# Values projected head by head, with the expert bias added as they leave PSUM

## The chip, the cores and the metric

The kernel runs on one core of a Trainium2 chip. The metric is the device time of one execution in microseconds (us), the median of several runs. A core has five engines that matter here: TensorE (PE) for matrix products and transposes, VectorE (DVE) and ScalarE (ACT) for elementwise work and for emptying PSUM, GpSimd (POOL) for elementwise work between tiles in SBUF, and SyncE (SP), which issues DMAs. Each engine has its own queue of instructions, and they meet at semaphores.

## The reference

A small vision tower: a tokenizer, attention with relu differences, an attention whose projections belong to experts, linear attention, and routed experts. The change is in the third. For 128 images (B) of 64 tokens (T) with 256 features (D), split into four chunks of 64 features, each chunk goes through four experts (e) with two heads each:

```python
gate = softmax(xn @ router_w.T + router_b)
qkv  = einsum('btcd,ekd->btcek', xc, qkv_w)          # xc: xn in four chunks c of 64
attn = softmax(einsum('bcehtd,bcehsd->bcehts', q, k) * scale)
y    = einsum('bcehts,bcehsd->bcehtd', attn, v)       # heads h side by side: 64 wide
y    = einsum('btced,eod->btceo', y, proj_w) + proj_b # proj_b: one bias per expert
out  = einsum('btceo,bte->btco', y, gate)
return residual + out.reshape(B, T, D) @ out_w.T
```

So the bias of expert e enters once, times the gate of e. The softmax weights of a head sum to one over the tokens s. A bias that is added to the values of one of the two heads of an expert therefore comes out of that head's sum as the same bias, and the gate that multiplies the weights multiplies it too.

## The kernel before

`expert_attention` works on pairs of images: 64 pairs, 128 tokens on the partitions, in blocks of four pairs. All tensors are fp32. The projection matrices are folded into the value matrices at the start (`wvp`), so that what leaves the mixing of the heads (`pz`) is already projected. The softmax weights are multiplied by the gates on POOL (`weights`, L987), so that the sum over the experts is made in PSUM by the four products that accumulate into one place of `pz`.

The loop over pairs is software-pipelined, and its order is written out by hand under `manual_schedule`: every engine takes its instructions in the order of the program's text. In step p three pairs are in work: `old` (p - 1) is transposed, mixed and added to the output; `cur` (p) gets its scores and its softmax; `new` (p + 1) gets queries, keys and values. In PE's order one step is: the first transposes of the old pair (L1001), the scores of the current one (L965), queries and keys of the new one (L933) with the old pair's other transposes between, the mixing `pz` (L1014), the values `pv` (L945), the output product `po` (L1028), and last the block work of the step. DVE takes in one step: for each of two halves of the scores a maximum (L977) and a subtraction (L978), then for each half a sum (L984) and a reciprocal (L985), with small work of the block between, then the copies of the values that are its own (L954), and last the addition of `po` to the running state `h2` (L1030). ACT copies queries and keys (L937), the transposed weights (L1004), makes the exponents (L981), copies `z` (L1022) and its share of the values (L954). POOL scales the weights (L991, L992) and normalises coming blocks (L866, L869).

The block work is put in the steps by `at`: a coming block's statistics are in DVE's part of the steps with p mod 4 of 1 and 2, the transposes of its normalised rows (L874) in PE's part of the steps 0 and 1, its router logits (L885) in step 2, the softmax of its gates (L892 to L904) in step 3.

[...] Two tiles of two banks are the scores; the other four banks are the pool `psq`, tag `pq`, in which everything else takes turns: a new tile takes the bank that was given back the longest ago. In one step they are taken in this order: two `pt`, two `pqk`, two `pt`, two `pqk`, `pz`, two `pv`, two `pv`, `po`, and then the tile of the block work, if the step has one.

Before the change, `values(fc)` makes the values of both heads for one half `fc` of the features, two tiles each time, with products of 256 columns. ACT copies those of `fc` 0, DVE those of `fc` 1. The bias takes a way of its own: the start of the stage multiplies it by `out_w` (`pb`, L819) and lays the result out in `bn`, four rows for each pair of a block; the gates of a block are transposed by PE (L908), copied by ACT into one of three `gT` tiles (L911), and each pair adds a third product to `po`:

```python
nc.tensor.matmul(po, self.blk.gT, bn[:, self.n, :], start=False, stop=True)
```

PE executes an fp32 product as two records in the trace, and a transpose as one.

Of the kernel before, what the change touches and what calls it, by code (L numbers as in the profile page):

```python
# [11 lines left out]
F32 = mybir.dt.float32  # L12
# [7 lines left out]
P = 128  # L20
B = 128
T = 64
D = 256
# [737 lines left out]
def expert_attention(c, hd, normw, wr, br, wqkv, wvT, wproj, bproj, wout):  # L761
# [3 lines left out]
    tc, nc, h2 = c.tc, c.nc, c.h2  # L765
    SCALE = float(1.0 / np.sqrt(np.float32(32)))
    NP = B // 2
    NB = 4
    with (
# [12 lines left out]
        brs = wp.tile([P, 4], F32, name="brs")  # L782
        nc.sync.dma_start(brs, br.partition_broadcast(P))
        w = wp.tile([P, 2 * D], F32, name="w")
        bp2 = wp.tile([P, 4], F32, name="bp2")
        for k in range(2):
            nc.sync.dma_start(w[k * 64 : k * 64 + 64, :], wqkv)
            nc.sync.dma_start(bp2[k * 64 : k * 64 + 64, :], bproj)
        wv = wp.tile([32, 8, 64], F32, name="wv")
        nc.scalar.dma_start(wv, wvT)  # L790
        wpj = wp.tile([32, 8, 64], F32, name="wpj")
# [10 lines left out]
        for k in range(2):  # L802
            for e in range(4):
                for h in range(2):
                    r = (e % 2 * 2 + h) * 64
                    nc.tensor.matmul(
                        pv[k * 64 : k * 64 + 64, e // 2, r : r + 64],
                        wv[:, e * 2 + h, :],
                        wpj[:, e * 2 + h, :],
                        start=True,  # L810
                        stop=True,
                    )
        wvp = wp.tile([P, 2, D], F32, name="wvp")
        nc.vector.tensor_copy(wvp, pv)


        pb = psq.tile([4, D], F32, tag="pq", name="pb")
        for fc in range(2):
            nc.tensor.matmul(pb, bp2, wo[:, fc, :], start=(fc == 0), stop=(fc == 1))  # L819
        b4 = wp.tile([4, D], F32, name="b4")  # L820
        nc.vector.tensor_copy(b4, pb)
        bn = wp.tile([P, NB, D], F32, name="bn")
        nc.gpsimd.memset(bn, 0.0)
        for n in range(NB):
            nc.sync.dma_start(bn[4 * n : 4 * n + 4, n, :], b4)
        gTs = [wp.tile([P, P], F32, name=f"gT{k}") for k in range(3)]
        for gT in gTs:
            nc.gpsimd.memset(gT, 0.0)

        class Block:  # L830

            def __init__(self, p0):
                self.p0, self.gT = p0, gTs[p0 // NB % 3]

            def statistics(self, n0):
                if n0 == 0:
# [63 lines left out]
            def gates(self):  # L903
                nc.gpsimd.tensor_mul(self.gate, self.gate, bcast(self.gm, 2, 4))  # L904

            def gates_transpose(self):
                self.pgt = psq.tile([4 * NB, P], F32, tag="pq", name="pgt")
                nc.tensor.transpose(self.pgt, self.gate.rearrange("p n e -> p (n e)"), c.ident)  # L908

            def gates_transposed(self):  # L910
                nc.scalar.copy(self.gT[0 : 4 * NB, :], self.pgt)  # L911

        class Pair:


            def __init__(self, p, blk):
                self.p, self.n, self.blk = p, p % NB, blk
                self.xT = blk.xT[:, :, p % NB, :]
                self.e, self.sm, self.pT = {}, {}, {}

                self.qk = vp.tile([P, 4, 2, 2, P], F32, tag="qk", name="qk", bufs=2)

                self.v = vp.tile([P, 4, 2, D], F32, tag="v", name="v")

            def queries_keys(self, fc):

# [9 lines left out]
                for par in range(2):  # L936
                    nc.scalar.copy(self.qk[:, 2 * fc + par], pq[par])  # L937

            def values(self, fc):
                pv = [psq.tile([P, 2, D], F32, tag="pq", name="pv") for _ in range(2)]  # L940
                for j in range(2):
                    for eh in range(2):
                        for par in range(2):
                            r = slice(par * 64, par * 64 + 64)
                            nc.tensor.matmul(  # L945
                                pv[par][eh * 64 : eh * 64 + 64, j, :],
                                self.xT[r, fc, j * 64 : j * 64 + 64],
                                wvp[r, eh, :],
                                start=True,
                                stop=True,  # L950
                            )
                for par in range(2):
                    copy = nc.scalar.copy if fc == 0 else nc.vector.tensor_copy
                    copy(self.v[:, 2 * fc + par], pv[par])  # L954

            def scores(self):

# [48 lines left out]
            def mixed(self):  # L1006

                pz = psq.tile([P, 2, P], F32, tag="pq", name="pz")
                for fc in range(2):
                    for j in range(2):  # L1010
                        t = slice(j * 64, j * 64 + 64)
                        for r in range(4):
                            for par in range(2):
                                nc.tensor.matmul(  # L1014
                                    pz[par * 64 : par * 64 + 64, fc, t],
                                    self.v[:, 2 * fc + par, j, r * 64 : r * 64 + 64],
                                    self.pT[r // 2][:, r % 2, 2 * fc + par, t],
                                    start=(r == 0),
                                    stop=(r == 3),
                                )  # L1020
                self.z = ep.tile([P, 2, P], F32, tag="z", name="z", bufs=2)
                nc.scalar.copy(self.z, pz)  # L1022

            def output(self):
                p = self.p
                po = psq.tile([P, D], F32, tag="pq", name="po")
                for fc in range(2):
                    nc.tensor.matmul(po, self.z[:, fc], wo[:, fc, :], start=(fc == 0), stop=False)  # L1028
                nc.tensor.matmul(po, self.blk.gT, bn[:, self.n, :], start=False, stop=True)
                nc.vector.tensor_add(h2[:, p], h2[:, p], po)  # L1030
                if p % 4 == 3:
                    nc.sync.dma_start(
                        hd[2 * p - 6 : 2 * p + 2].rearrange("(n b) t f -> (b t) n f", b=2),
                        h2[:, p - 3 : p + 1],
                    )
# [5 lines left out]
        def at(n, place, f, *a):  # L1041
            key = (n, place) if n >= 0 else "first"
            work.setdefault(key, []).append(lambda: f(*a))

        for b, x in enumerate(blocks):
            n = NB * b
            at(n - 11, "DVE", x.statistics, 0)
            at(n - 10, "DVE", x.statistics, 2)
            at(n - 9, "POOL", x.factors)
            for k in range(NB):  # L1050
                at(n - 8 + k, "POOL", x.normal, k)
            at(n - 4, "PE", x.transpose, 0)
            at(n - 3, "ACT", x.transposed, 0)
            at(n - 3, "PE", x.transpose, 1)
            at(n - 2, "ACT", x.transposed, 1)
            at(n - 2, "PE", x.logits)
            at(n - 1, "DVE", x.logits_less_max)
            at(n - 1, "ACT2", x.exponents)
            at(n - 1, "DVE2", x.sums)
            at(n - 1, "POOL", x.gates)  # L1060
            at(n, "PE", x.gates_transpose)
            at(n + 1, "ACT", x.gates_transposed)

        def do(key):
            for step in work.pop(key, ()):
# [3 lines left out]
        with tc.manual_schedule():  # L1069
            old, cur = None, Pair(0, blocks[0])  # L1070
            for fc in range(2):
                cur.queries_keys(fc)
                cur.values(fc)
            for p in range(NP):
                new = Pair(p + 1, blocks[(p + 1) // NB]) if p + 1 < NP else None
                do((p, "ACT"))
                if old:
                    old.transposed(0)
                cur.scores()
                cur.less_max(0)  # L1080
                cur.less_max(1)
                if new:
                    new.queries_keys(0)
                if old:
                    old.transposed(1)
                cur.exponents(0)
                if new:
                    new.queries_keys(1)
                cur.exponents(1)
                cur.sums(0)  # L1090
                cur.weights(0)
                do((p, "DVE"))
                do((p, "ACT2"))
                cur.sums(1)
                cur.weights(1)
                do((p, "DVE2"))
                do((p, "POOL"))
                if old:
                    old.mixed()
                if new:  # L1100
                    new.values(0)
                    new.values(1)
                if old:
                    old.output()
                do((p, "PE"))
                old, cur = cur, new
            for x in range(2):
                old.transposed(x)
            old.mixed()
            do((NP, "ACT"))  # L1110
            old.output()
        assert not work

# [873 lines left out]
def layout(**i):  # L1987
# [32 lines left out]

    o["wvf"] = w[:, 2].reshape(8, 32, 64).transpose(1, 0, 2)
    o["wproj"] = i["L0_ffn_proj_w"].reshape(4, 64, 2, 32).transpose(3, 0, 2, 1).reshape(32, 8, 64)
    o["bproj"] = i["L0_ffn_proj_b"].T
    o["wout"] = i["L0_ffn_out_w"].T

    q, k, v = (i[f"L1_attn_W{n}"].T.reshape(D, 8, 32).transpose(0, 2, 1).reshape(D, D) for n in "qkv")
# [29 lines left out]
```

## Time and profile before

What | us
--- | ---
median of 3 runs | 2745.43 (2745.28 to 2745.86)
the profiled execution | 2744.63
its span, first to last instruction | 2742.5
PE busy in the span | 2598.4 (95%)
DVE, ACT, POOL busy | 2027.9, 1623.1, 1633.7
stage of this change, about 1139 to 1942 | 803
PE busy over 1400 to 1900, in its middle | 494.87 of 500

A row of the profile's groups gives line, engine, operation, the tiles out and in, the number of instructions, then busy time and mean duration, and last the idle time of the engine before them. A row of the timeline gives start, duration, engine, line and operation, and merges like neighbours. A row of the waits says which engine at which line waited for which other, how long in total, how often, and the longest. PEld is PE's weight load, which runs beside the products.

### The profile page before, as it was taken

Reading aid. Unit: us, or ns where it says so; the run is one execution under the profiler, and the core shown is the slowest. Engines: PE = TensorE matmul, PEld = TensorE weight load, DVE = VectorE, ACT = ScalarE, POOL = GpSimd, SP = SyncE. Lnnn points to the kernel's source line nnn. Section 1 sums busy time; section 2 is a strip of 40 time slices with the busy share of each in tenths; the row PEclk is TensorE's granted clock in tenths of the full one; section 3 lists DMA queues with packets and bytes.
Section 4 is the critical chain, followed back from the end, with each engine's and each line's share of the span. In section 5 each row is a group of like instructions: output and inputs, shape, how many; then the busy total and the mean of one; then the engine's idle time right before and its main releaser. Section 6 shows DMA issues by size and latency. Waiting matters only on the chain. (4 is left out here: it accounts for less than half of the span.)

```text
span 2742.5 us, 77026 instructions
## 1 busy us (share of the span) xinstructions
PE 2598.4 (95%) x33309; PEld 1733.3 (63%) x33309; DVE 2027.9 (74%) x3025; ACT 1623.1 (59%) x3414; POOL 1633.7 (60%) x1390
## 2 busy tenths in 40 slices
PE   7989999999999999799999999999699986999997
PEld 4553444444344443588888888888466565888886
DVE  5759999999998989477777777777467776444443
ACT  2228888888888888366656666666355543233332
POOL 3328888888888889656566656553233212454444
PEclk9999999999999999899999999999899998999998
DMA  3000000000000000000000000000333454555554
GB/s 109 32 12 1 2 1 2 2 2 2 1 2 1 2 2 1 12 11 19 11 11 19 11 11 18 11 12 17 96 83 85 100 118 149 179 198 197 184 195 134
DMA packets 138015, 140.83 MB, mean 51 GB/s; under 512 B 107747, under 2 KB 121461, under 8 KB 129984
## 3 DMA queue, kind: packets, MB, share of 16 engines
q1 hardware_dynamic: 126928, 117.95, 14.2%
q0 software_dynamic: 7648, 14.77, 1.7%
q8 instruction: 263, 4.31, 0.6%
q10 hardware_dynamic: 3088, 3.08, 0.4%
q14 instruction: 88, 0.72, 0.1%
HBM read 103.96 MB, written 32.54 MB: 50 GB/s over the span
## 5 line engine op out<-in xcount | busy, mean ns | idle before, releaser
L525 POOL TENSOR_TENSOR m<-q,k 128x1024 f32<-128x1024 f32 x384 | 719.0, 1904 | 31.7 <-PE sc L327 16.3
L517 DVE TENSOR_TENSOR m<-pc,k 128x2048 f32<-128x2048 f32 (+1 forms) x320 | 646.7, 2058 | 0.5 <-ACT q L461 0.5
L327 PE MATMUL sc<-m,wide 128*32 128x512 f32 x4096 | 529.7, 599 | 12.0 <-DVE m L517 7.1
L526 ACT ACTIVATE m<-m 128x1024 f32<-128x1024 f32 x384 | 402.5, 1050 | 5.9 <-POOL m L525 5.4
L327 PEld LDWEIGHTS sc<-m,wide 128*32 128x32 f32 x4096 | 126.6, 109 | 259.6 <-issue 146.2
L535 ACT ACTIVATE m<-k,q 128x64 f32<-128x64 f32 x1024 | 271.0, 339 | 0.8 <-DVE k L408 0.8
L977 DVE TENSOR_REDUCE mx<-sc 128x16 f32<-128x1024 f32 x128 | 156.0, 1219 | 153.2 <-PE sc L965 138.1
L992 POOL TENSOR_TENSOR e<-e,mx 128x1024 f32<-128x1024 f32 x128 | 243.4, 1902 | 10.1 <-POOL mx L991 0.2
L937 ACT COPY qk<-pqk 128x512 f32<-128x512 f32 x256 | 139.0, 604 | 132.2 <-PE pqk L933 132.1
L991 POOL TENSOR_TENSOR mx<-mx,gate 128x16 f32<-128x16 f32 x128 | 27.6, 216 | 314.8 <-ACT z L1022 144.3
L1886 PE MATMUL ph<-xt,w1s 128*128 128x256 f32 x896 | 198.8, 380 | 3.6 <-DVE xt L1877 2.6
L1902 PE MATMUL po<-w2s,hT 128*128 128x256 f32 x896 | 198.0, 379 | 0.0
L1004 ACT COPY pT<-pt 128x512 f32<-128x512 f32 x256 | 138.6, 599 | 99.0 <-PE pt L1001 98.3
L1886 PEld LDWEIGHTS ph<-xt,w1s 128*128 128x128 f32 x896 | 169.8, 190 | 28.2 <-DVE xt L1877 3.2
L1902 PEld LDWEIGHTS po<-w2s,hT 128*128 128x128 f32 x896 | 168.1, 190 | 21.7
L933 PE MATMUL pqk<-xT,w 64*128 64x128 f32 x2048 | 169.6, 289 | 3.7 <-issue 3.5
L978 DVE TENSOR_TENSOR e<-sc,mx 128x1024 f32<-128x1024 f32 x128 | 156.7, 1224 | 4.4
L1920 POOL DMA_INDIRECT out<-y,rout x56 | 56.7, 1013 | 167.8 <-ACT hT L1890 124.8
L933 PEld LDWEIGHTS pqk<-xT,w 64*128 64x128 f32 x2048 | 142.3, 189 | 21.1 <-issue 12.0
L984 DVE TENSOR_REDUCE mx<-e 128x16 f32<-128x1024 f32 x128 | 153.3, 1198 | 2.1 <-ACT e L981 2.0
L1890 ACT ACTIVATE hT<-ph,w1s 128x256 f32<-128x256 f32 x224 | 93.0, 470 | 96.9 <-PE ph L1886 96.9
L1001 PE MATMUL pt<-ident,e 128*128 128x128 f32 x1024 | 141.5, 278 | 5.8 <-POOL e L992 2.8
(308 smaller groups left out, 4958.7 us busy)
## 6 DMA issues: line engine op xcount, KB each, us to landing
w1s<-in_we SPq DMA_DIRECT2D x30, 1028.0 KB, 5.0
w2s<-in_we SPq DMA_DIRECT2D x30, 1024.0 KB, 5.2
hd<-h SPq DMA_DIRECT2D x16, 512.0 KB, 3.4
x<-hd SPq DMA_DIRECT2D x16, 512.0 KB, 5.7
h<-hd SPq DMA_DIRECT2D x4, 2048.0 KB, 12.6
hx<-h SPq DMA_DIRECT2D x4, 2048.0 KB
out<-h SPq DMA_DIRECT2D x4, 2048.0 KB, 20.6
xt<-in_x SPq DMA_DIRECT2D x15, 512.0 KB, 3.5
```

The costliest lines, as they stand in the source:

```text
L327: nc.tensor.matmul(dst[j : j + 32], wide[:, hf, s : s + 32], part, start=start, stop=stop)
L517: nc.vector.tensor_tensor(m, bcast(self.pq[:, hf, i : i + n], 3, T), k, ALU.max)
L525: nc.gpsimd.tensor_tensor(m, bcast(self.q[:, hf, s : s + 2], 3, T), k, ALU.subtract)
L526: nc.scalar.activation(m, m, AF.Relu)
L535: nc.scalar.activation(self.parts[i, hf][:, q], self.blk.k[:, hf, i], AF.Relu, bias=self.q[:, hf, i - NB // 2, q : q + 1], scale=-1.0,)
L933: nc.tensor.matmul(pq[par][:, k, eh, :], w[r, f : f + P], self.xT[r, fc], start=True, stop=True)
L977: nc.vector.tensor_reduce(mx, sc, AX.X, ALU.max)
L978: nc.vector.tensor_sub(e, sc, bcast(mx, 2, T))
L984: nc.vector.tensor_reduce(self.sm[x], self.e[x], AX.X, ALU.add)
L992: nc.gpsimd.tensor_mul(e, e, bcast(sm, 2, T))
L1886: nc.tensor.matmul(ph[:, j], self.w1[:, w0 : w0 + P], self.xt[:, fc], start=(fc == 0), stop=(fc == 1))
L1902: nc.tensor.matmul(po, self.hT[:, f, r * P : r * P + P], self.w2[:, f, :], start=(f == 0), stop=(f == 7))
```

## The change

The values are made head by head. The folded value matrix `wvp` is laid out with head 0 of all experts in its first 128 columns and head 1 in the others, and `values(h)` makes one head for both halves of the features, two tiles each time, with twice as many products of half as many columns. The value tile in SBUF has a new order of its axes, and the mixing reads it accordingly. The two tiles of head 0 leave PSUM by DVE, as an addition of the bias `bv`; the two of head 1 by ACT, as copies. `bv` is loaded by two DMAs in place of the two of `bp2`: each expert's bias broadcast over the 64 partitions that hold that expert's tokens. Gone are the transposes of the gates, their copies, `gT`, `bn`, `b4`, the products `pb`, the four DMAs that fill `bn`, and the third product of `po`.

```diff
-        bp2 = wp.tile([P, 4], F32, name="bp2")
+        bv = wp.tile([P, P], F32, name="bv")
         for k in range(2):
             nc.sync.dma_start(w[k * 64 : k * 64 + 64, :], wqkv)
-            nc.sync.dma_start(bp2[k * 64 : k * 64 + 64, :], bproj)
+            nc.sync.dma_start(
+                bv[k * 64 : k * 64 + 64, :],
+                bproj[2 * k : 2 * k + 2].rearrange("e o -> (e o)").partition_broadcast(64),
+            )
...
-                    r = (e % 2 * 2 + h) * 64
+                    r = (h * 2 + e % 2) * 64
...
-        pb = psq.tile([4, D], F32, tag="pq", name="pb")
-        for fc in range(2):
-            nc.tensor.matmul(pb, bp2, wo[:, fc, :], start=(fc == 0), stop=(fc == 1))
-        b4 = wp.tile([4, D], F32, name="b4")
-        nc.vector.tensor_copy(b4, pb)
-        bn = wp.tile([P, NB, D], F32, name="bn")
-        nc.gpsimd.memset(bn, 0.0)
-        for n in range(NB):
-            nc.sync.dma_start(bn[4 * n : 4 * n + 4, n, :], b4)
-        gTs = [wp.tile([P, P], F32, name=f"gT{k}") for k in range(3)]
-        for gT in gTs:
-            nc.gpsimd.memset(gT, 0.0)
...
-            def gates_transpose(self):
-                self.pgt = psq.tile([4 * NB, P], F32, tag="pq", name="pgt")
-                nc.tensor.transpose(self.pgt, self.gate.rearrange("p n e -> p (n e)"), c.ident)
-
-            def gates_transposed(self):
-                nc.scalar.copy(self.gT[0 : 4 * NB, :], self.pgt)
...
-                self.v = vp.tile([P, 4, 2, D], F32, tag="v", name="v")
+                self.v = vp.tile([P, 2, 2, 4, P], F32, tag="v", name="v")
...
-            def values(self, fc):
-                pv = [psq.tile([P, 2, D], F32, tag="pq", name="pv") for _ in range(2)]
-                for j in range(2):
-                    for eh in range(2):
-                        for par in range(2):
-                            r = slice(par * 64, par * 64 + 64)
-                            nc.tensor.matmul(
-                                pv[par][eh * 64 : eh * 64 + 64, j, :],
-                                self.xT[r, fc, j * 64 : j * 64 + 64],
-                                wvp[r, eh, :],
-                                start=True,
-                                stop=True,
-                            )
+            def values(self, h):
+                pv = [psq.tile([P, 4, P], F32, tag="pq", name="pv") for _ in range(2)]
+                for fc in range(2):
+                    for j in range(2):
+                        for eh in range(2):
+                            for par in range(2):
+                                r = slice(par * 64, par * 64 + 64)
+                                nc.tensor.matmul(
+                                    pv[par][eh * 64 : eh * 64 + 64, 2 * fc + j, :],
+                                    self.xT[r, fc, j * 64 : j * 64 + 64],
+                                    wvp[r, eh, h * P : h * P + P],
+                                    start=True,
+                                    stop=True,
+                                )
                 for par in range(2):
-                    copy = nc.scalar.copy if fc == 0 else nc.vector.tensor_copy
-                    copy(self.v[:, 2 * fc + par], pv[par])
+                    if h == 0:
+                        nc.vector.tensor_add(self.v[:, par, 0], pv[par], bcast(bv, 1, 4))
+                    else:
+                        nc.scalar.copy(self.v[:, par, 1], pv[par])
...
-                                    self.v[:, 2 * fc + par, j, r * 64 : r * 64 + 64],
+                                    self.v[:, par, r % 2, 2 * fc + j, r // 2 * 64 : r // 2 * 64 + 64],
...
-                    nc.tensor.matmul(po, self.z[:, fc], wo[:, fc, :], start=(fc == 0), stop=False)
-                nc.tensor.matmul(po, self.blk.gT, bn[:, self.n, :], start=False, stop=True)
+                    nc.tensor.matmul(po, self.z[:, fc], wo[:, fc, :], start=(fc == 0), stop=(fc == 1))
...
-            at(n, "PE", x.gates_transpose)
-            at(n + 1, "ACT", x.gates_transposed)
...
-            do((NP, "ACT"))
```

The loop itself still calls `new.values(0)` and then `new.values(1)`, after `old.mixed()` and ahead of `old.output()`.

More of the change, by code (lines that the diff above doesn't have):

```diff
@@ L814, in expert_attention @@
         nc.vector.tensor_copy(wvp, pv)
-        pb = psq.tile([4, D], F32, tag="pq", name="pb")
-        for fc in range(2):
-            nc.tensor.matmul(pb, bp2, wo[:, fc, :], start=(fc == 0), stop=(fc == 1))
-        b4 = wp.tile([4, D], F32, name="b4")
-        nc.vector.tensor_copy(b4, pb)
-        bn = wp.tile([P, NB, D], F32, name="bn")
-        nc.gpsimd.memset(bn, 0.0)
-        for n in range(NB):
-            nc.sync.dma_start(bn[4 * n : 4 * n + 4, n, :], b4)
-        gTs = [wp.tile([P, P], F32, name=f"gT{k}") for k in range(3)]
-        for gT in gTs:
-            nc.gpsimd.memset(gT, 0.0)
         class Block:
             def __init__(self, p0):
-                self.p0, self.gT = p0, gTs[p0 // NB % 3]
+                self.p0 = p0
             def statistics(self, n0):
@@ L2022, in layout @@
     o["wproj"] = i["L0_ffn_proj_w"].reshape(4, 64, 2, 32).transpose(3, 0, 2, 1).reshape(32, 8, 64)
-    o["bproj"] = i["L0_ffn_proj_b"].T
+    o["bproj"] = i["L0_ffn_proj_b"]
     o["wout"] = i["L0_ffn_out_w"].T
```

## The prediction, made before the change was run

> **What bounds the kernel now.** I read the page's slices first, then busy time by stage, then the waits, then one pair in the timeline. The expert attention runs from about 1139 to 1942 us of the span. In its steady part TensorE (PE) is busy 494.9 of 500 us at the full granted clock; VectorE (DVE) 386.4, ScalarE (ACT) 309.6, GpSimd (POOL) 285.1. The columns are stretch, length, then PE, PE weight loads, DVE, ACT, POOL, clock, DMA share, GB/s:
> ```profile
> 1400.00:1900.00 500.00, 494.87 (x11375) 418.32 (x11373) 386.39 (x554) 309.58 (x561) 285.11 (x315) 1.00 0.04 14
> ```
> So PE's own queue is the bound, and 1% of slack is left. What decides the change is how near other engines stand to PE at the place that it touches. The waits of this stage name that place:
> ```profile
> PEld po L1028 <- ACT v L954: 23.5, 61, 0.4
> DVE mx L977 <- PE sc L965: 137.9, 57, 3.7
> ```
> The first line: in 61 pairs the output product `po` takes the PSUM buffer that the first value tile leaves. `psq` has four, and the order of use is `pz`, four value tiles, `po`. It costs nothing yet (0.4 us of weight loads, in which PE drains the values' products anyway). The second: DVE waits each pair for the scores, so DVE's chain begins anew at each pair's scores, and nothing carries over. One pair (number 32), from the values to the next scores:
> ```profile
> 1544.91 2.10 PE L945 MATMUL pv<-wvp,xT 64*64 64x256 f32 x32
> 1545.47 0.39 ACT L1022 COPY z<-pz 128x256 f32<-128x256 f32 x1
> 1545.57 0.25 DVE L985 RECIPROCAL mx<-mx 128x16 f32<-128x16 f32 x1
> 1545.74 1.16 DVE L984 TENSOR_REDUCE mx<-e 128x16 f32<-128x1024 f32 x1
> ...
> 1546.05 1.07 ACT L954 COPY v<-pv 128x512 f32<-128x512 f32 x2 [0.19 <-PE pv L945]
> ...
> 1546.93 1.13 PE L1028 MATMUL po<-wo,z 128*128 128x256 f32 x4
> 1546.94 0.25 DVE L985 RECIPROCAL mx<-mx 128x16 f32<-128x16 f32 x1
> 1547.11 1.23 DVE L954 COPY v<-pv 128x512 f32<-128x512 f32 x2
> ...
> 1547.90 0.59 PE L1029 MATMUL po<-bn,gT 128*128 128x256 f32 x2
> ...
> 1548.33 0.27 PE L908 MATMUL pgt<-ident,gate 128*16 128x128 f32 x1
> ```
> ACT empties the first two value tiles from 1546.05, 0.9 us before `po` starts. DVE comes to its two only at 1547.11, after the second sum and reciprocal: later than `po`'s start. Today that is harmless, since `po` doesn't ask for those.
>
> **What the Trainium skill says.** "TensorE: Matmul & The Clock Gate", section "Part 2: What happens when you issue a matmul": matmuls stay in program order, only weight loads are pulled ahead. So everything behind a waiting `po` waits too; the trace agrees, since the transposes of the next pair start only after L1029. The same page, Part 1 ("What's actually happening"): the clock is halved after an idle window of some 3.4 us. PE has such idle at this stage's start, where the granted clock over 1112 to 1139 is 0.62; in the loop it is 1.00. "VectorE: DVE Perf Modes", "The perf-mode tier table": an fp32 tensor_tensor, or any fp32 operation with a PSUM operand, gets no faster mode. The trace agrees: L499, an fp32 add of 128x512 from PSUM, takes 0.677 us, the copies at L954 0.662.
>
> **The change, part by part.**
>
> *Removed from PE.* A record of 256 columns takes 0.216 us of PE's time: the two of L1029 start at 1547.90 and the next instruction at 1548.33, 0.43 for both. There are 64 such products: 64 x 0.432 = 27.6 us. The 16 gate transposes take 0.11 each (1548.33 to 1548.44): 1.7. Together 29.4 us of PE.
>
> *Values by head.* Before: 32 records of 256 columns in four 64x64 quarters of the array, 8 rounds x 0.216 = 1.73 us. After: 64 records of 128 columns, 16 rounds x 0.109 (as the 128-column transposes of L874) = 1.75. Fewer than 16 rounds are excluded. From above: a round now has four weight loads of 64 columns in 0.109; L1014 does two such loads in a round of 0.063 (1542.89 to 1544.91, 32 rounds), so four take at most 0.126, 2.02 us in all, 0.29 more than now. I take 0.02; either is covered by the wait worked out next, of at least 0.9. Without that cover the upper bound costs 18 us over 63 pairs.
>
> *The eviction trades engines.* The same four 128x512 tiles leave PSUM. But the first two (head 0) now leave by DVE with the bias, the last two by ACT. So `po`, in the built program too, waits for DVE's first add where it waited for ACT. DVE's place for it is unchanged: after two maxima and subtractions, sum, reciprocal, the block's small work, sum, reciprocal. For one block of four pairs, S is the start of the scores (L965); times after S:
>
> pair mod 4 | scores to first L977 | first `v` on DVE starts | ends | `po` starts now
> 2 (statistics, logits) | 1.63 | 10.25 | 10.88 | 9.02
> 3 (softmax of gates) | 1.63 | 10.10 | 10.79 | 9.99
> 0 (plain) | 1.63 | 9.20 | 9.83 | 9.02
> 1 (statistics) | 1.63 | 10.32 | 10.95 | 9.02
>
> To the end I add 0.05 us for the add against the copy (0.677 against about 0.63 in the first of each two) and 0.05 for the signal (DVE's L894 ends at 1533.96, and the product that waits for it loads at 1534.02). So `po` moves to 10.98, 10.9, 9.93 and 11.05: later by 1.96, 0.90, 0.91 and 2.03. I took the same difference in each pair 1 to 62 (0 has no `po`; 63 makes no new values). It sums to 80.9 us: 53.7 in the 32 pairs of the first and last kind (the last three of each have no statistics and lose 0.9; a few already start `po` late), 27.2 in the other 30. The delay isn't given back: after `po` PE must do the transposes and the next scores before DVE can start again, and both then run at today's distances.
>
> *Behind the waiting `po`:* `ptx` or the logits, the transposes `pt`, the next scores; DVE and, through it, ACT and POOL wait for those. The next buffer after `po` needs DVE's second add, 0.6 after the first; `po` itself takes 0.86, so it is covered. DVE's L1030 ends some 1.6 after `po`'s start, the next scores are ready no sooner than 3.5 after: covered. ACT copies head 1 about 1 us later than now, done at S + 10.2, before `pt` needs the buffer at S + 10.8. POOL's scaled weights are there at S + 10.2 and S + 12.5, and are needed later too. Uncovered, each would cost at most some 0.3 us a pair.
>
> *Setup and ends.* POOL loses the memsets of `bn` (0.95) and three `gT` (0.49), which hold up the first factors at 1114.68; these then wait for DVE's moments, ready at 1114.33: 0.35 us less. Four `bn` issues of 0.6 us leave SP's queue and two products `pb` PE's, both beside POOL's normalisation, worth nothing. The two `bv` loads stand where the `bp2` loads stood (0.59 us of issue each, done by about 1119), and are first used past 1134. The first pair's PE waits some 0.2 for DVE's adds. The 16 ACT copies of the gates (0.25 each) were in ACT's idle time: nothing.
>
> *Sum:* 80.9 - 29.4 - 0.35 + 0.2 = +51.3 us. The profiled execution took 2744.63 (span 2742.5, and 2.1 around it), 0.8 below the median, within 0.03%: 2745 + 51 gives 2796.
>
> **The rivals.**
> 1. *PE stays the bound*, because `po`'s buffer comes free in time or the change gives it another: then only the removed work counts, 29.4 + 0.15 - 64 x 0.02, about -28 us: 2717. For it: PE is 99% busy. Against it: the wait of L1028 on the first value tile in 61 pairs, and DVE starting on that tile 0.1 to 1.3 us after `po`'s present start. The point that decides: the delay is 1.30 us a pair on the average (80.9 / 62), the removed work 0.46 (29.4 / 64); with DVE there 0.84 us earlier the change would neither gain nor lose.
> 2. *The delay, and the clock with it.* PE would idle 0.9 to 2.0 of each 12 to 15 us. If the granted clock fell to 0.93, as over the 1000 to 1138 stretch, the PE work inside the loop (from `po` to the first maximum, 4.3 us) grows by 0.32 a pair: +20 more, 2816. Against it: idle stretches of 2.6 us near 1930 left the clock at 1.00.
> 3. *Only part of the delay*, if DVE reaches the adds sooner because ACT's exponents do: ACT has no copies of values ahead of the next pair's `qk`. But the exponents come after PE's `pqk`, tied to S, and bind only in plain pairs: L984 waits for them 2.0 us in the whole stage. With the 0.05 for the add absent too (3 us): +46, 2791.
>
> That the biases or values differ in cost from what is said leaves no other time: the counts of products and evictions are as told.
>
> **How the numbers follow.** Main case with rival 3: 0.85, at 2784 to 2808 (0.2 us a pair, 63 pairs, either way, for the add, the signal and POOL). Rival 2: 0.08. Rival 1: 0.07, of which 0.05 ends faster and the rest within 0.2% (5.5 us, about what a measurement can tell from no change). Leaving out rival 1 and the upper half of rival 2, the range is 2780 to 2813. Slower: 0.93.
>
> **What would show it.** In the profile after: L1029 and L908 gone; a wait of `po`'s weight load for `v` on DVE, 0.9 to 2.0 us each, 80 us in all, in some 62 pairs; PE busy down to about 90% of the loop (11.8 us of 13.2 a pair); pairs of about 13.7, 14.7, 12.8 and 12.3 us where they take 12.2, 13.1, 12.4 and 11.9; DVE's wait for the scores unchanged or longer. Wrong if `po` starts at S + 9.0 with the add not done, or if the clock in the loop is below 1.00.

## The result, and the profile after

The change made the kernel slower: 2822.2 us (median of four executions, 2816.3 to 2822.4) against 2745.6, a ratio of 1.0274 (95% interval 1.0256 to 1.0292). That is +76.6 us where +51 was forecast: the sign and the wait as told, the size outside the range. The execution that was profiled took 2816.3 us (span 2814.6), the lowest of the four; its loop is 72.3 us longer than before, from the first scores to the last (856.4 against 784.1), so all of the loss lies there.

Two views show that there are two losses. The first is the table by stretch, with the columns of the prediction's first fence; below the middle of the loop stand stretches cut where the clock changes, three around one fall and two around another:

```profile
1400.00:1900.00 500.00, 450.92 (x11320) 402.21 (x11319) 350.76 (x507) 279.41 (x498) 271.52 (x306) 0.95 0.04 13
1553.67:1557.08 3.41, 2.78 (x90) 2.47 (x86) 3.31 (x8) 2.22 (x5) 1.66 (x2) 1.00 0.02 5
1557.08:1560.49 3.41, 2.21 (x16) 2.11 (x17) 2.12 (x5) 0.48 (x1) 3.11 (x4) 1.00 0.00 0
1560.49:1567.32 6.83, 6.83 (x158) 6.32 (x157) 1.71 (x2) 1.17 (x2) 1.91 (x2) 0.50 0.01 2
1669.69:1673.10 3.41, 3.07 (x24) 2.97 (x25) 1.30 (x3) 0.00 (x0) 3.23 (x4) 1.00 0.02 5
1673.10:1676.51 3.41, 3.41 (x137) 2.96 (x134) 0.00 (x0) 1.17 (x2) 1.15 (x1) 0.50 0.00 0
```

PE is busy 451 of 500 us instead of 495: it stands still for 49 us where it did for 5. And the granted clock over these 500 us is 0.95 where it was 1.00: after a stretch of 3.41 us in which PE shows only 16 records and 2.21 us of busy time, it is 0.50 for 6.83 us. At 1673.10 it halves although the profile counts PE as busy for 3.07 of the 3.41 us before; 1.84 us of these are the router's 16 records, of 4 columns each.

The waits name the first loss, in the place that the prediction gave:

```profile
DVE mx L966 <- PE sc L954: 190.0, 62, 6.8
...
PEld po L1017 <- DVE v L941: 86.3, 61, 2.2
ACT v L943 <- PE pv L932: 72.9, 61, 1.5
PE po L1017 <- DVE v L941: 71.6, 61, 1.9
```

`po` waits 61 times for DVE's first add, up to 1.9 us. ACT, which used to empty the first tiles, now waits for the second ones. DVE's wait for the scores has grown from 137.9 to 190.0 us: both engines now wait for each other in turn. Pair 32, the one shown of before, in the timeline after:

```profile
1583.84 2.11 PE L932 MATMUL pv<-wvp,xT 64*64 64x128 f32 x64
1584.41 0.39 ACT L1011 COPY z<-pz 128x256 f32<-128x256 f32 x1
...
1584.68 1.16 DVE L973 TENSOR_REDUCE mx<-e 128x16 f32<-128x1024 f32 x1
...
1585.88 0.25 DVE L974 RECIPROCAL mx<-mx 128x16 f32<-128x16 f32 x1
1585.99 1.07 ACT L943 COPY v<-pv 128x512 f32<-128x512 f32 x2 [1.19 <-PE pv L932]
1586.05 1.22 DVE L941 TENSOR_TENSOR v<-pv,bv 128x512 f32<-128x512 f32 x2
1586.73 0.73 PEld L1017 LDWEIGHTS po<-wo,z 128*128 128x128 f32 x4 [1.02 <-DVE v L941]
1586.73 1.13 PE L1017 MATMUL po<-wo,z 128*128 128x256 f32 x4 [0.78 <-DVE v L941]
...
1587.70 0.60 PE L865 MATMUL ptx<-ident,xn 128*128 128x128 f32 x4
```

The 64 short records of the values take as long as the 32 long ones (2.11 against 2.10 us). DVE reaches its adds only after the second reciprocal; the first add ends at 1586.68, and `po` starts 0.05 later. Its scores began at 1576.84, so this is S + 9.89 (forecast 9.93). Pair 30, with statistics and the logits, shows the same wait and then the second loss:

```profile
1557.60 1.22 DVE L941 TENSOR_TENSOR v<-pv,bv 128x512 f32<-128x512 f32 x2
...
1558.28 1.13 PE L1017 MATMUL po<-wo,z 128*128 128x256 f32 x4 [1.83 <-DVE v L941]
...
1559.25 2.30 PE L876 MATMUL pg<-wrs,xT 128*128 128x4 f32 x16
...
1561.40 1.95 PE L990 MATMUL pt<-ident,e 128*128 128x128 f32 x8
...
1563.28 2.26 PE L954 MATMUL sc<-qk 32*64 32x64 f32 x128
...
1565.47 2.02 PE L918 MATMUL pqk<-xT,w 64*128 64x128 f32 x16
```

From 1560.49 on, the transposes take 1.95 us, the scores 2.26, `pqk` 2.02. One step later, at full clock again, the same work takes 1.04, 1.59 and 1.16:

```profile
1575.88 1.04 PE L990 MATMUL pt<-ident,e 128*128 128x128 f32 x8
...
1576.85 1.59 PE L954 MATMUL sc<-qk 32*64 32x64 f32 x128
...
1578.37 1.16 PE L918 MATMUL pqk<-xT,w 64*128 64x128 f32 x16
```

The slowed work lies between `po` and DVE's next maximum or just behind it, so the pair is 1.3 us longer than its like at full clock, and the next one 0.9. The trace has 14 stretches of half clock in the loop, of 3.4 to 10.2 us, 68.3 us together. Each begins in a step with p mod 4 of 1 or 2, the two with statistics, 11 to 14 us after the scores: just behind the long wait.

From one start of the scores to the next, most common value, in us:

p mod 4 | before | forecast | after, at full clock
--- | --- | --- | ---
0 (plain) | 11.94 | 12.3 | 12.25
1 (statistics) | 12.19 | 13.7 | 13.38
2 (statistics, logits) | 13.13 | 14.7 | 14.61
3 (softmax of gates) | 12.36 | 12.8 | 12.63

### The profile page after: what moved, and what is told of

Read it like the earlier page. It is cut to its first block, busy times and chain, and to the rows that moved or that the text cites. A ratio compares the mean times of both kernels' runs of the same rounds, so it can differ in the third digit from the quotient of the medians.

```text
span 2814.6 us, 80786 instructions
## 1 busy us (share of the span) xinstructions
PE 2601.7 (92%) x35209; PEld 1774.6 (63%) x35209; DVE 2027.8 (72%) x3024; ACT 1622.4 (58%) x3398; POOL 1633.1 (58%) x1386
## 5 line engine op out<-in xcount | busy, mean ns | idle before, releaser
L990 PE MATMUL pt<-ident,e 128*128 128x128 f32 x1024 | 153.4, 294 | 5.3 <-POOL e L981 2.8
```

The lines of the kernel that those rows point to most:

```text
L990: nc.tensor.transpose(pt[:, cq, :], e[:, i : i + 2, :].rearrange("p e s -> p (e s)"), c.ident)
```

## The experiments

**The removed work alone.** The kernel before, with only this taken out of each step (the bias is left out of the sum):

```diff
-                    nc.tensor.matmul(po, self.z[:, fc], wo[:, fc, :], start=(fc == 0), stop=False)
-                nc.tensor.matmul(po, self.blk.gT, bn[:, self.n, :], start=False, stop=True)
+                    nc.tensor.matmul(po, self.z[:, fc], wo[:, fc, :], start=(fc == 0), stop=(fc == 1))
...
-            at(n, "PE", x.gates_transpose)
-            at(n + 1, "ACT", x.gates_transposed)
...
-            do((NP, "ACT"))
```

> The kernel before without the third product of po, the gates' transposes and their copies; the bias is left out. Theory 1 (the change loses by po's wait for DVE's first add, and by half-clock windows that this wait sets off; what it removes is worth its PE time): PE loses 29.4 us, but in the 13 pairs with p mod 4 = 1 and statistics the transposes already wait for DVE's second-pair copies, so some 5 us of it stay: about 2721, clock 1.00 in the loop. Theory 2 (the removed work was hidden, and the shorter products of the values are what costs): 2740 to 2746.

Measured: 2727.0 us, ratio 0.9936 (0.9920 to 0.9953). The removed work is worth 18 us here, not 29. The plain steps fall to 11.39 and the others to 12.70 and 11.92, all by about what was taken out; those with p mod 4 of 1 and statistics stay at 12.19. There the transposes `pt` take a bank that DVE's value copies still hold, and the wait takes the place of the product:

```profile
PE pt L1001 <- DVE v L954: 4.9, 10, 0.5
```

That is half of what is missing against 29.4; the rest is in scattered steps that are 0.3 to 1.6 us longer, of which this run has more than before. What lengthens them stays open.

**The engines of the copies alone.** The kernel before, all its products kept:

```diff
-                    copy = nc.scalar.copy if fc == 0 else nc.vector.tensor_copy
+                    copy = nc.vector.tensor_copy if fc == 0 else nc.scalar.copy
```

> The kernel before with nothing changed but the engines of the value copies: DVE takes the first two tiles, ACT the last two. Theory 1: po waits for DVE as after the change, with all removed work still in: about +72 us of wait at full clock, and the half-clock windows on top (27 us in the kernel after), 2830 to 2850; a wait of L1028 for L954 on DVE of 0.9 to 2.0 us in some 61 pairs. Theory 2: no wait arises, 2745. If the wait is there but the clock stays at 1.00, about 2817.

Measured: 2817.6 us, ratio 1.0261 (1.0244 to 1.0278): +72.5, the value named for the wait without the clock. This one line brings the wait. The waits, in the same columns as above:

```profile
PEld po L1028 <- DVE v L954: 99.7, 61, 2.4
...
PE po L1028 <- DVE v L954: 71.9, 61, 1.9
```

PE's wait is that of the kernel after (71.6). Yet half-clock time in the loop is 10 us instead of 68: waits of this length seldom halve the clock by themselves. The two kernels end within 5 us of each other, although the change takes 29.4 us of PE work out: it loses about as much again by half clock, which the filled runs below price at some 30 us.

**The order of the two heads.** The kernel after, with ACT's tiles first:

```diff
-                    new.values(0)
                     new.values(1)
+                    new.values(0)
```

> The kernel after with new.values(1) called ahead of new.values(0): ACT's copies of head 1 come first, DVE's adds second, so po takes a bank that ACT gives back. Everything else as after. Theory 1: the wait and the half-clock windows go, the removed work counts; pairs with p mod 4 = 1 gain little, since their transposes wait for DVE's adds: about 2722, and close to the run without the bias product. Theory 2 (shorter products): no better than 2745, with the values taking longer on PE. Theory 3 (the add itself is dear on DVE): slower than the run without the bias product by over 10 us.

Measured: 2729.7 us, ratio 0.9940 (0.9924 to 0.9957). The wait for DVE at `po` is gone, one stretch of half clock of 3.4 us is left in the loop, and the kernel is 92 us faster than the kernel after by an exchange of two lines. It stands 2.7 us from the run without the bias product, within the spread of either: the short products and the add cost nothing that these runs can tell. Of DVE only this is left in PE's waits, for the transposes:

```profile
PE pt L990 <- DVE v L941: 4.8, 10, 0.5
```

**PE's wait filled.** The kernel after, with the products of head 1 repeated into the same tiles in the steps with the long waits (`self.n` is the new pair's, one ahead of p). The added products write the same values once more.

```diff
-                for fc in range(2):
+                twice = 2 if h == 1 and self.n in (2, 3) else 1
+                for fc in [0, 1] * twice:
```

> The kernel after, with head 1's products made twice into the same tiles in the steps whose new pair has p mod 4 of 2 or 3, those that hold the long waits: 32 times 16 products, about 28 us more work for PE, in which it would wait. Theory 1: the extra work lies in the wait and keeps the clock up; no half-clock window in the loop, and the time falls by 15 to 27 us against the kernel after, to 2790 to 2806. If the half clock has another cause than PE's idle time, the time stays at 2816 to 2822. Theory 2 (PE's values are the bound): the time rises by 28 us to about 2850.

Measured: 2804.9 us, ratio 1.0221 (1.0204 to 1.0238). With 28 us more work for PE, the kernel is 17 us faster than the kernel after. Not all half clock is gone: four stretches are left in the steps, all with p mod 4 of 2 (20.5 us), none with 1. So a third repetition there:

```diff
+                times = {2: 2, 3: 3}.get(self.n, 1) if h == 1 else 1
+                for fc in [0, 1] * times:
```

> The kernel after, with head 1's products made twice in steps with p mod 4 = 1 and three times in steps with p mod 4 = 2: 42 us more work for PE than the kernel after, 14 more than the run with two everywhere (2804.9, which kept half-clock windows only in steps with p mod 4 = 2). Theory 1: no half-clock window is left in the loop's 62 steps, the full-clock pairs stay at 12.25, 13.38, 14.61, 12.63 us, and the time is 2788 to 2797, below both. If PE's amount of work decided: 2815 or more.

Measured: 2792.2 us, ratio 1.0166 (1.0149 to 1.0183). The stretch table of this run, to be read beside that of the kernel after:

```profile
1400.00:1900.00 500.00, 472.41 (x12683) 423.55 (x12681) 363.64 (x524) 289.24 (x518) 280.40 (x316) 1.00 0.05 14
```

The clock is 1.00, no stretch of half clock is left before the last pair, and the pairs stand at 12.26, 13.38, 14.61 and 12.64 us: those of the kernel after at full clock, with 42 us more work in them. The work lies in PE's wait, which shrinks from 71.6 us:

```profile
PE po L1018 <- DVE v L942: 33.0, 43, 1.0
```

This run puts a price on each loss: the wait for DVE, net of the work removed, is +47 us, and the half clock the other 30. These are differences of medians; the profiled executions of the two kernels differ by 22 us, and that of the kernel after is its fastest.

**The statistics out of DVE's way.** The kernel after, with the statistics of a coming block behind the addition of `po`:

```diff
-            at(n - 11, "DVE", x.statistics, 0)
-            at(n - 10, "DVE", x.statistics, 2)
+            at(n - 11, "LATE", x.statistics, 0)
+            at(n - 10, "LATE", x.statistics, 2)
...
                     old.output()
+                do((p, "LATE"))
                 do((p, "PE"))
```

> The kernel after, with the statistics of a coming block moved on DVE from ahead of the second sum to behind the addition of po, where DVE waits for the next scores. Theory 1 (wait for DVE's first add, plus half-clock windows where PE streams too little): the waits of 1.9 to 2.0 us in 26 steps shrink to 0.9, all pairs stand as the plain ones do in the kernel after at full clock (12.25, 12.25, 13.55, 12.63 us), which is 17 us above before: 2762, and up to 10 more if the logits' steps still fall to half clock. If the half clock came from any wait at all, some 27 more: 2789. If DVE's order had nothing to do with it: 2816 to 2822.

Measured: 2768.2 us, ratio 1.0080 (1.0063 to 1.0096), 54 us below the kernel after. All pairs take the values forecast for this run (12.26, 12.26, 13.56, 12.63), so the length of DVE's queue ahead of the add is what `po` waits for. In the trace 10 us of half clock are left in steps of the steady part, both stretches with p mod 4 of 2, and 6.8 in the first step.

**Both edits.**

> Both edits: new.values(1) ahead of new.values(0), and the statistics behind the addition of po. Theory 1: with ACT's copies first po does not wait, and with the statistics gone the transposes in steps with p mod 4 = 1 no longer wait for DVE's adds (12.19 to about 11.45 us, 13 times, 10 us): 2718 to 2722, faster than the kernel with head 1 first alone (2729.7). If those transposes wait for something else: 2727 to 2731.

Measured: 2717.5 us, ratio 0.9903 (0.9886 to 0.9919): the fastest of all, just below the 2718 to 2722 that were expected of theory 1. Steps with p mod 4 of 1 fall from 12.19 to 11.41, PE's wait for DVE is gone, and PE is the bound again, at full clock:

```profile
1400.00:1850.00 450.00, 442.87 (x11688) 396.59 (x11681) 359.66 (x521) 284.60 (x512) 272.56 (x302) 1.00 0.05 14
```

**Wider logits.** What remained in steps with p mod 4 of 2 pointed at the router's products, which come after `po` there: 16 records spaced by their weight loads, each with only 4 columns to stream. The kernel after, with 60 columns of zeros added:

```diff
-        wrs = wp.tile([P, 2, 4], F32, name="wrs")
-        nc.sync.dma_start(wrs, wr.rearrange("(c p) e -> p c e", p=P))
+        wrs = wp.tile([P, 2, 64], F32, name="wrs")
+        nc.gpsimd.memset(wrs, 0.0)
+        nc.sync.dma_start(wrs[:, :, 0:4], wr.rearrange("(c p) e -> p c e", p=P))
...
-                self.pg = pg = psq.tile([P, NB, 4], F32, tag="pq", name="pg")
+                self.pg = pg = psq.tile([P, NB, 64], F32, tag="pq", name="pg")
```

(the softmax reads columns 0 to 3 of each).

> The kernel after, with the router's products (L876 there) made 64 columns wide instead of 4, the weights of the other 60 being zero. Each of their records is spaced by its weight load of 128 columns (0.11 us), so at full clock their time should not change. It asks why half-clock windows fall mostly into steps with p mod 4 = 2, where these products follow the long wait. Theory 1a (the clock goes by how much of a window PE streams columns, and a 4-column product counts almost as idle): half-clock time in those steps falls from 47 us to under 20, the total to 2800 to 2812. Theory 1b (any product counts as work, only the wait itself matters): no change, 2816 to 2822.

Measured: 2805.8 us, ratio 1.0232 (1.0206 to 1.0257), 16 below the kernel after, at 14.61 us for such a pair at full clock as before the edit; one of its four executions took 2816.2, as long as the fastest of the kernel after. Half-clock time in these steps fell from 47.8 to 20.5 us. It also fell in the steps with p mod 4 of 1, from 20.5 to 10.2, which the edit doesn't touch; so part of the difference between two single traces is chance. The run speaks for theory 1a without settling it.

## Why the prediction was right and wrong

- *PE is the bound before, and `po` takes the bank of the first value tile:* right. The swap of engines alone cost 72 us, the exchange of two lines took the whole loss away.
- *`po` moves to DVE's first add:* right. S + 10.94 and 9.89 in pairs 30 and 32 against 10.98 and 9.93; adds and copies both have a median duration of 0.68 us on DVE. The wait net of the removed work is +47 us (the filled run) where the sum gave +51.
- *The 4 us between these:* two places of the sum were too dear. In steps with p mod 4 of 1 it kept today's distance from `po` to the next scores, 3.17 us, less the product: 2.74. But some 0.4 us of that distance was itself a wait of `pt` for DVE's value copies, and it is gone once `po` waits for DVE: 2.37 in the run at full clock. So these pairs grew by 1.19 us, not 1.60: 13 pairs, 5 us. In steps with p mod 4 of 3 the adds begin at S + 9.99 and not at 10.10, so `po` starts at 10.70 where 10.9 was forecast: 3 us in all. Scattered longer steps gave part of this back.
- *The step that failed:* "both then run at today's distances". It took the work behind the delayed `po` at full clock, and left the clock to a rival of chance 0.08. Rival 2 is what happened, on top of the main case: 30 us of the 77. It had the mechanism, but not the price. It spread a clock of 0.93 evenly over the loop, +20; the mean over the middle of the loop is 0.95, but the half clock comes in stretches just behind the long waits, where PE's work decides when the next pair can start.
- *Why the clock was dismissed:* "TensorE: Matmul & The Clock Gate", Part 1, has the clock drop after an idle window of some 3.4 us. The measurement differs: no wait for DVE in this loop is longer than 2.2 us, PE shows 2.21 us of busy time in the first window shown and 3.07 in the second, and the clock halved. The stretch of 2.6 us near 1930 that left the clock at 1.00 is one sample of where a wait can fall; the loop offers 26 long waits. And the kernel before shows falls without a wait of 3.4 us too. At this stage's start, which the prediction read as such an idle, PE's longest wait before the clock halves at 1117.34 is 2.64 us (1113.17 to 1115.81); at 2233.49, in another stage, it halves behind a wait of 2.14 us:

```profile
1113.93:1117.34 3.41, 1.53 (x29) 1.56 (x30) 2.61 (x12) 0.00 (x0) 3.10 (x11) 1.00 0.70 156
...
2230.08:2233.49 3.41, 1.27 (x12) 0.97 (x13) 3.34 (x5) 2.17 (x8) 1.26 (x1) 1.00 0.86 218
2233.49:2236.90 3.41, 3.41 (x66) 3.41 (x68) 3.41 (x28) 0.00 (x0) 1.62 (x1) 0.50 0.29 74
```

- *Values by head cost nothing:* right, 2.11 us against 2.10, and 2729.7 against 2727.0 for the kernel that lacks them.
- *The work behind the waiting `po`:* right in that no second wait appeared. *Setup:* the first scores start 0.97 us earlier, POOL's first memset of the stage already 0.50: the rest, 0.47, stands against 0.15 forecast. The runs cannot tell these apart: with the setup of the kernel after, the first scores start anywhere between 1136.86 and 1139.19.

## What to carry to other kernels

When PSUM banks go round as here, the engine that empties the first tile of a group decides when PE may take its next one. So ask not how long the eviction takes but what stands ahead of it in that engine's queue, and give the first tiles to the engine that is early. A saving on the engine that is the bound is only worth having while that engine stays the bound; here the exchange of the two heads made the change a gain of 15 us against the kernel before, and the later statistics brought it to 27, of the 29 that the removed work had promised. Late statistics were not tried on the kernel before, so what part of the last 12 us belongs to the change is not shown. And price a new wait on PE with the clock in it.

## What the runs showed of the hardware

PE's clock fell by half although PE never stopped for a whole 3.41 us. Half-clock stretches in these loops last 3.41, 6.83 or 10.24 us, multiples of 3.41. To see what precedes them I cut the loop into windows of 3.41 us that end where such stretches begin, and estimated from the starts of PE's records what share of each window PE streams columns: 0.84 ns a column (0.216 us for 256), overlapping records counted once, so that the 4-column logits count almost nothing.

- Before: from the first scores to the last, the lowest window at full clock has 0.47, and none is followed by half clock. The stretch near 1930 that the prediction relied on lies behind the last scores; its lower window has 0.38.
- After: the 14 windows that are followed by half clock have 0.26 to 0.41, and only four others are as low. The one before 1673.10, with PE busy for 3.07 us, has 0.37.
- With the waits filled more, no window after the first step is below 0.42, and the clock stays at 1.00.

The estimate doesn't give a clean limit. The run with swapped copies has a dozen windows of 0.38 to 0.39 that stay at full clock, and two, of 0.39 and 0.42, that do not; in the run with head 1 first a window of 0.46 is followed by half clock. What the chip counts exactly stays open. That work put into waits of 2 us keeps the clock up, and that without it the clock can halve, is shown by the filled runs.
